# Queries and keys of two head sets from one product each, with the values' projection and a portion of filler moved

## The chip, the cores and the metric

The kernel runs on one core of a Trainium2 chip. The metric is the device time of one execution in microseconds; three runs of the kernel before gave 748.2, 746.93 and 748.02, with a median of 748.02 us. Engines are named as the profile names them: PE (TensorE), DVE (VectorE), ACT (ScalarE), POOL (GpSimd) and SP, which issues most of the transfers.

## What is computed

Two transformer layers over 16 sequences of 256 tokens with 128 features. The change touches the attention of the first layer alone. Cut to that:

```python
xn = _layernorm(x)
qvk = (xn @ Wqvk).reshape(b, s, 3, H, HD)          # H = 16 heads of HD = 8
q, v, k = (qvk[:, :, 0], qvk[:, :, 1], qvk[:, :, 2])
scores = jnp.einsum('bshi,bthi->bsth', q, k)
scores = (scores + mask[None, :, :, None]) / math.sqrt(d)      # causal
weights = jax.nn.softmax(scores, axis=2)
wv = jnp.einsum('bsth,bthi->bshi', weights, v).reshape(b, s, d)
x = x + wv @ Wo + ...                               # and a layer of experts, then a second layer
```

The experts of the first layer, and the retention and experts of the second, run between and after the attention of the sequences.

## The kernel before

**Heads on partitions.** The 16 heads form two sets (s = 0, 1) of eight, and a set lies on the 128 partitions as four groups (j) of 32 rows. A group holds two heads (a = 0, 1), each of 8 rows. A head's score is a product with 32 rows of contraction, and the two heads of a group share the rows of the keys `kU`; the queries `qM` are kept once for each a, with the other head's rows zero. One more row of each group carries the maximum: 1 in `kU`, and the negative row maximum in `qM`. So the product `wts` gives scores with the maximum taken off.

**Making them (lines 418 to 440).** The padded weights `wqk` hold a block of 128 columns for queries or keys and for each set, with 16 of 32 columns used in every group. `products` makes four products a sequence, 128 x 256 each: two into the PSUM bank `pq`, two into `pk`. `keys_and_queries` takes them out: two ACT instructions of 512 columns for `qM`, scaled by a mask `qm`, and one for `kU`, which adds the 1 (`kone`) in row 16. For sequence 0 this last one is on DVE.

**The loop over sequences (lines 1526 to 1571).** Iteration n computes the maxima of sequence n+1 (`top`, with DVE's maximum `nm`) beside the weights of sequence n (`wts`, with the exponential on ACT and the causal select on POOL, both writing `pt`), in six steps. Then comes what I call the seam: the products of sequence n+2 (`project`), the transposes of the maxima `nm` of n+1 into `pm` with their copy `mT` on DVE and four transfers of SP into the rows of `qM` (`top_rows`), the values' projection `pv` of n+2 with its copy `va` on DVE (`project_v`), the two products `av` with the weights (`values`, one for each set, copied by ACT to `sv` and sent out to `num` and `dd`), the division `wv` on DVE (`divide`) that needs the denominators `den` of sequence n-1, and the output projection `po` of n-1, added to `x` by DVE (`project_out`).

**Filler.** All other work (normalization, routing, the first layer's experts, the second layer's steps, loads of weights) is cut into portions; `fill` issues the next portion. There are eight calls in an iteration: one after each of the six steps, one after the second `values`, one after `project_out`. So portion 8n+6 is the one after the second `values`.

**What sets the order.** Instructions go through wrappers (`InOrder`, line 164) that chain them: each engine executes in the order in which this program issues, and SP and POOL issue their transfers in that order too. PSUM is one pool of eight banks handed out in turn (`bank`, line 158).

Line numbers in the profile are mostly 173, the line of the wrapper, so instructions are told apart by the tile that they write and read.

Of the kernel before, what the change touches and what calls it, by code (L numbers as in the profile page):

```python
# [12 lines left out]
F32 = mybir.dt.float32  # L13
BF16 = mybir.dt.bfloat16
I32 = mybir.dt.int32
AF = mybir.ActivationFunctionType
ALU = mybir.AluOpType
AX = mybir.AxisListType
# [3 lines left out]
P = 128  # L22
# [20 lines left out]
def two_layer_kernel(  # L43
# [26 lines left out]
    B, S, D = h.shape  # L70
# [10 lines left out]
    w1pool = ctx.enter_context(tc.tile_pool(name="w1pool", bufs=1))  # L81
    dram = ctx.enter_context(tc.tile_pool(name="dram", bufs=1, space=DRAM))

    def bc(ap, shape):
        return ap.to_broadcast(list(shape))
# [3 lines left out]
    wqvk_sb = w1pool.tile([P, 3 * D], F32)  # L89
# [68 lines left out]
    def bank(shape, name="sc"):  # L158
        return ps.tile(shape, F32, tag="sc", name=name)
# [38 lines left out]
    pe, dve, act, pool, sp = (InOrder(e) for e in (nc.tensor, nc.vector, nc.scalar, nc.gpsimd, nc.sync))  # L198

    def matmul(*args, **kw):  # L200
        return pe.matmul(*args, **kw)

    def transpose(*args):
        return pe.transpose(*args)
# [7 lines left out]
    xnT = big.tile([P, N], F32)  # L212
# [77 lines left out]
    def fill_with(o, value):  # L290
        act.activation(
            o.rearrange("p (k n) -> p k n", n=P),
            bc(ones[0 : o.shape[0]].unsqueeze(1), [o.shape[0], o.shape[1] // P, P]),
            AF.Copy,
            scale=value,
        )


    wqk = w1pool.tile([P, 2, 2, P], F32)
    fill_with(wqk.rearrange("p n s r -> p (n s r)"), 0.0)  # L300


    vas = [w1pool.tile([P, 2, 8, 32], F32, name=f"va{k}") for k in range(3)]
# [17 lines left out]
    for n, c0 in ((0, 0), (1, 2 * D)):  # L321
        for s in range(2):
            dve.tensor_copy(
                wqk[:, n, s, :].rearrange("p (j r) -> p j r", j=4)[:, :, 0:16],
                wqvk_sb[:, c0 + 64 * s : c0 + 64 * s + 64].rearrange("p (j r) -> p j r", j=4),
            )

    r32 = w1pool.tile([P, 32], F32)
    dve.tensor_reduce(r32, ident.rearrange("p (j r) -> p r j", j=4), AX.X, ALU.add)
    km = w1pool.tile([P, 2], F32)  # L330
    dve.tensor_reduce(km, r32[:, 0:16].rearrange("p (a r) -> p a r", a=2), AX.X, ALU.add)
    qm = w1pool.tile([P, 2], F32)
    dve.tensor_scalar(qm, km, 1.0 / math.sqrt(D), None, ALU.mult)
    kone = r32[:, 16:17]

    for t in range(2, 8):
        ln_stats(mv0, t, t)
# [79 lines left out]

    def project(n):

        return keys_and_queries(n, *products(n))  # L420

    def products(n):
        cols = slice(S * n, S * n + S)
        pq = bank([P, 2, S], "pq")
        pk = bank([P, 2, S], "pk")
        for m, o in ((0, pq), (1, pk)):
            for s in range(2):
                matmul(o[:, s, :], lhsT=wqk[:, m, s, :], rhs=xnT[:, cols], start=True, stop=True)
        return pq, pk

    def keys_and_queries(n, pq, pk):
        kU = wk.tile([P, 2, S], F32, tag="kU", name="kU")
        qM = wk.tile([P, 2, 2, S], F32, tag="qM", name="qM")
        for a in range(2):
            act.activation(qM[:, :, a, :], pq, AF.Copy, scale=qm[:, a : a + 1])
        if n == 0:
            dve.tensor_scalar(kU, pk, kone, None, ALU.add)
        else:
            act.activation(kU, pk, AF.Identity, bias=kone)
        return kU, qM, vas[n % 3]  # L440

    def project_v(n):
        pv = bank([P, 2, P], "pv")
        for t in range(2):
            matmul(
                pv[:, t, :],
                lhsT=xnT[:, S * n + t * P : S * n + t * P + P],
                rhs=wqvk_sb[:, D : 2 * D],
                start=True,
                stop=True,  # L450
            )
        va4 = vas[n % 3].rearrange("p k h (d a) -> p (k h) d a", a=4)
        dve.tensor_copy(va4[:, :, :, 0:2], pv.rearrange("p k (h a d) -> p (k h) d a", a=2, d=8))
# [34 lines left out]
    def top_rows(ops, nm):  # L488

        qM = ops[1]  # L490
        pm = bank([16, S], "pm")
        for c in range(2):
            transpose(pm[:, c * P : c * P + P], nm[:, c, :], ident)
        mT = wk.tile([16, S], F32, tag="mT", name="mT")
        dve.tensor_copy(mT, pm)
        for s in range(2):
            for a in range(2):
                h0 = 8 * s + 4 * a
                sp.dma_start(qM[16:P:32, s, a, :], mT[h0 : h0 + 4, :])

    def weights(ops, u, js, pts):

# [51 lines left out]
    def values(ops, s, pts, num, dd):  # L554

        va = ops[2]
        av = bank([P, 2, S], "av")
        for j in range(4):
            matmul(
                av[32 * j : 32 * j + 32].rearrange("p a q -> p (a q)"),  # L560
                lhsT=va[:, 0, 4 * s + j, :],
                rhs=pts[1 + s][:, j, :],
                start=True,
                stop=False,
            )
        for j in range(4):
            matmul(
                av[32 * j : 32 * j + 32, :, P:S],
                lhsT=va[:, 1, 4 * s + j, :],
                rhs=pts[0][:, j, 256 * s : 256 * s + 256].rearrange("p (a q) -> p a q", a=2),  # L570
                start=False,
                stop=True,
            )

        sv = wk.tile([P, 2, S], F32, tag="sv", name="sv")
        act.copy(sv, av)
        sp.dma_start(dd[8 * s : 8 * s + 8, :].rearrange("(a j) q -> j a q", a=2), sv[2:P:32, :, :])
        for a in range(2):
            r = slice(64 * s + 32 * a, 64 * s + 32 * a + 32)
            sp.dma_start(num[r, :], sv[a:P:4, a, :])  # L580
# [641 lines left out]
    def after(portion, *gens):  # L1222
        return [portion, [g for g in gens]]
# [8 lines left out]
    def fill():  # L1232
        for start, gens in beside:
            while gens and start <= at["portion"]:
                try:
                    next(gens[0])
                    break
                except StopIteration:
                    gens.pop(0)
        at["portion"] += 1  # L1240
# [236 lines left out]
    def turn(us):  # L1477

        end()
        at["us"] += us  # L1480
        while at["us"] > 0 and other:
            cost, what, i = other[0]
            if i not in done:
                at["us"] = 0.0
                return
            other.pop(0)
            end()
            what(i)
            at["us"] -= cost
# [11 lines left out]
    ops = {}  # L1501
# [11 lines left out]
    early = products(1)  # L1513
# [2 lines left out]
    dve.tensor_scalar(rev, eid, -1.0, float(E), ALU.mult, ALU.add)  # L1516
    dve.tensor_reduce(hm16, ident.rearrange("p (g j r) -> p j g r", g=4, j=2), AX.XY, ALU.add)
    dve.tensor_reduce(blk16, ident.rearrange("p (h r) -> p h r", h=H1), AX.X, ALU.add)
    ops[1] = keys_and_queries(1, *early)
    project_v(1)  # L1520
    load_router()
    for i in range(2):
# [3 lines left out]
    for n in range(B):  # L1526
        pts = {}
        num = wk.tile([P, S], F32, tag="num", name="num")
        dd = dram.tile([H0, S], F32, tag="dd", bufs=3, name="dd")
        if n + 1 < B:  # L1530
            maxima[n + 1] = wk.tile([P, 2, 16], F32, tag="nm", name="nm")
        sums = denominators(prev[1]) if prev is not None else iter(())
        if n + 1 == B:
            turn(4.0)
        for u in range(3):
            for js, others in (((0, 1), (2, 3)), ((2, 3), (0, 1))):
                parts = [weights(ops[n], u, others, pts)]
                if n + 1 < B:
                    parts.insert(0, top(ops[n + 1], u, js, maxima[n + 1]))
                together(*parts)  # L1540
                next(sums, None)
                fill()
                if n + 1 == B:
                    turn(2.0)
        if n + 2 < B:
            ops[n + 2] = project(n + 2)
        if n + 2 < B:
            top_rows(ops[n + 1], maxima[n + 1])
            project_v(n + 2)
        values(ops[n], 0, pts, num, dd)  # L1550
        if n + 2 == B:
            top_rows(ops[n + 1], maxima[n + 1])
        if prev is not None:
            wv = divide(prev[0], held["den"])
        values(ops[n], 1, pts, num, dd)
        if n + 1 == B:
            held["dens"] = denominators(dd)
            next(held["dens"])
        fill()
        if prev is not None:  # L1560
            project_out(n - 1, wv)
        prev = num, dd
        if n + 1 == B:
            turn(2.0)
        fill()
        if n + 1 == B:
            turn(2.0)
        if n == 8:
            fW1_sb = big.tile([P, E, FF], F32, tag="WV", name="fW1_sb")
            fW2_sb = big.tile([P, E, NFC, D], F32, tag="xnw", name="fW2_sb")  # L1570
            beside.append(after(0, load1()))
# [108 lines left out]
```

## Time and profile before

The profiled execution took 747.65 us; its span, from the first to the last instruction, is 745.9 us.

| | |
|---|---|
| median of three runs | 748.02 us |
| profiled execution, its span | 747.65 us, 745.9 us |
| granted TensorE clock, mean | 0.991 |
| attention of the 16 sequences | from about 7 to about 400 us |
| products pq and pk of one sequence | 8 records, 1.83 us from the first to the next work's start |
| ACT qM, kU, 512 columns each | 684 ns, 695 ns |
| DVE copies mT, va | 0.41 us, 0.43 us |

A line of the timeline gives the start in microseconds from the span's start, the time until the last of a merged run of instructions ends, the engine, the operation with out<-in, the shape and the count; in brackets stands how long the engine had been idle and what released it. Records of TensorE overlap, so the time from one start to the next is what a product costs.

### The profile page before, as it was taken

To read this page: it belongs to the slowest core of one execution; us is meant where nothing else is said; L and a number is where in the kernel's file an instruction comes from. 1 tells how busy PE (TensorE), PEld (TensorE's weight loads), DVE (VectorE), ACT (ScalarE), POOL (GpSimd) and SP (SyncE) were. 2 spreads that over 40 slices of the span, in tenths; PEclk is the share of its full clock that TensorE was granted. 3 is DMA by queue.
4 is the path that set the end of the run, shared out by engine and by line. 5 is a ranking of instruction groups with operands and counts; after the bars stand their busy time and mean duration, and the time that the engine had idled before them with its cause. 6 is when DMAs were issued, how large, how long until landed. Compare 5 with 4: busy or idle time off the path is not lost.

```text
span 745.9 us, 14847 instructions
## 1 busy us (share of the span) xinstructions
PE 716.3 (96%) x5645; PEld 478.9 (64%) x5648; DVE 397.2 (53%) x1066; ACT 361.3 (48%) x714; POOL 274.5 (37%) x475
## 2 busy tenths in 40 slices
PE   8899989999899999999999899999999999999997
PEld 6557556766555666656565566666776676767675
DVE  8675876766657666586452656753323233223222
ACT  5477535555576676876666444233232322232222
POOL 1253345787556557666372413344000000121000
PEclk9899999999999999999999999999999999999999
DMA  4114464233333645413222121232000000323111
GB/s 125 23 57 130 131 188 117 39 47 43 52 73 88 153 104 142 88 36 54 65 51 56 23 65 43 80 79 35 1 29 2 0 1 1 43 34 38 35 38 43
DMA packets 79312, 45.73 MB, mean 61 GB/s; under 512 B 17112, under 2 KB 74656, under 8 KB 79232
## 3 DMA queue, kind: packets, MB, share of 16 engines
q1 hardware_dynamic: 62432, 34.84, 16.3%
q0 software_dynamic: 16800, 9.83, 10.3%
q8 instruction: 50, 0.82, 0.5%
q14 instruction: 30, 0.25, 0.1%
HBM read 24.97 MB, written 17.31 MB: 57 GB/s over the span
## 4 chain that ended last, share of the span: by engine, by line
PE 75%; DVE 12%; DMA 4%; POOL 3%; ACT 3%; issue 2%; SPq 1%; DVEq 0%; ACTq 0%; POOLq 0%
PE py L173 20%; PE ph L173 18%; PE top L173 8%; PE av L173 5%; PE wts L173 4%; DVE nm L173 4%; PE po L173 3%; PE pq L173 2%; DMA x<-ytab 2%; PE pk L173 2%; PE pret L173 2%; PE psc L173 1%; PE plog L173 1%; PE pb L173 1%; DVE st L173 1%
## 5 line engine op out<-in xcount | busy, mean ns | idle before, releaser
L173 ACT ACTIVATE hT<-ph,b1T 128x512 f32<-128x512 f32 (+1 forms) x134 | 90.1, 678 | 169.7 <-PE ph L173 154.0
L173 PEld LDWEIGHTS py<-fW_sb,hT 128*128 128x128 f32 x1328 | 155.2, 192 | 21.3 <-issue 19.8
L173 PE MATMUL py<-fW_sb,hT 128*128 128x128 f32 x1328 | 157.7, 276 | 0.0
L173 PE MATMUL ph<-xnT,fW_sb 128*128 128x512 f32 x320 | 147.4, 601 | 0.0
L173 DVE TENSOR_REDUCE nm<-top 128x2 f32<-128x512 f32 (+1 forms) x192 | 122.3, 681 | 32.6 <-PE wts L173 19.1
L173 ACT ACTIVATE pt<-wts 128x512 f32<-128x512 f32 x192 | 104.8, 599 | 66.3 <-PE wts L173 48.6
L173 PE MATMUL wts<-qM,kU 32*128 32x512 f32 (+1 forms) x512 | 121.2, 530 | 0.7 <-DVE come L173 0.5
L173 POOL TENSOR_SCALAR_AFFINE_SELECT pt<-pt 128x512 f32<-128x512 f32 (+1 forms) x96 | 82.7, 884 | 100.2 <-ACT pt L173 93.1
L173 PE MATMUL top<-kU,qM 32*128 32x256 f32 (+1 forms) x1024 | 110.9, 349 | 0.5 <-issue 0.4
L173 PEld LDWEIGHTS ph<-xnT,fW_sb 128*128 128x128 f32 x320 | 58.0, 192 | 61.9 <-issue 57.4
L173 PEld LDWEIGHTS top<-kU,qM 32*128 32x128 f32 x1024 | 73.6, 190 | 30.1 <-issue 26.5
L173 DVE SCALAR_TENSOR_TENSOR x<-py,gate,x 128x128 f32<-128x128 f32 x160 | 48.6, 346 | 70.7 <-PE py L173 70.7
L173 DVE TENSOR_SCALAR hT<-ph,b1T 128x512 f32<-128x512 f32 (+1 forms) x38 | 26.6, 708 | 96.7 <-ACT hT L173 58.1
L173 POOL DMA_DIRECT2D x<-acc x8 | 10.4, 1366 | 157.9 <-issue 115.0
L173 PEld LDWEIGHTS wts<-qM,kU 32*128 32x128 f32 x512 | 48.7, 189 | 7.5 <-DVE nm L173 2.1
L173 POOL TENSOR_SCALAR_AFFINE_SELECT s<-s 128x1024 f32<-128x1024 f32 x32 | 34.7, 1109 | 37.5 <-ACT s L173 37.5
L173 PE MATMUL av<-pt,va 128*32 128x256 f32 (+1 forms) x512 | 45.1, 489 | 2.5 <-POOL pt L173 2.1
L173 PE MATMUL top<-cmask,ident_bf 128*128 128x256 bf16 (+1 forms) x189 | 44.5, 316 | 0.5 <-DVE nm L173 0.5
L173 ACT COPY s<-psc 128x512 f32<-128x512 f32 x64 | 32.7, 602 | 4.7 <-PE psc L173 4.7
L173 PEld LDWEIGHTS av<-pt,va 128*32 128x32 f32 x512 | 14.7, 109 | 27.6 <-issue 19.7
L173 ACT COPY sv<-av 128x512 f32<-128x512 f32 x32 | 18.5, 590 | 24.4 <-issue 10.5
L173 PE MATMUL pq<-xnT,wqk 128*128 128x256 f32 (+1 forms) x80 | 26.5, 445 | 1.4 <-ACT xnT L173 1.4
(251 smaller groups left out, 932.7 us busy)
## 6 DMA issues: line engine op xcount, KB each, us to landing
ytab<-zeros SPq DMA_DIRECT2D x16, 256.0 KB
x<-ytab POOLq DMA_DIRECT2D x16, 256.0 KB
fW_sb<-in_L_ffn_W_dram SPq DMA_DIRECT2D x16, 256.0 KB
xtab<-xnw SPq DMA_DIRECT2D x8, 272.0 KB
num<-sv SPq DMA_DIRECT2D x64, 32.0 KB
den<-di SPq DMA_DIRECT2D x16, 128.0 KB
xtab<-xn SPq DMA_DIRECT2D x8, 256.0 KB
acc<-zeros SPq DMA_DIRECT2D x8, 256.0 KB
```

Source lines behind the costliest of these rows:

```text
L173: ins = f(*args, **kw)
```

## The change

Queries of both sets come out of one product, keys out of another: the columns of `wqk` interleave the sets and heads (row 4d + 2s + a in a group), all 128 columns are used, and masks pick what belongs to a set and head when the product is taken out. For queries there are four masks (one for each s and a); for keys a mask per set clears the row that carries the 1 and adds it. That row is 2 for set 0 and 0 for set 1. Both products go into one PSUM bank, `pqk`. They are taken out in six instructions of 256 columns. At the seam `project_v` goes ahead of `top_rows`, and the filler portion 8n+6 goes between the first and the second `values`, for n = 0 to 13.

```diff
-    wqk = w1pool.tile([P, 2, 2, P], F32)
-    fill_with(wqk.rearrange("p n s r -> p (n s r)"), 0.0)
+    wqk = w1pool.tile([P, 2, P], F32)
...
             dve.tensor_copy(
-                wqk[:, n, s, :].rearrange("p (j r) -> p j r", j=4)[:, :, 0:16],
-                wqvk_sb[:, c0 + 64 * s : c0 + 64 * s + 64].rearrange("p (j r) -> p j r", j=4),
+                wqk[:, n, :].rearrange("p (j d s a) -> p s j a d", j=4, s=2, a=2)[:, s],
+                wqvk_sb[:, c0 + 64 * s : c0 + 64 * s + 64].rearrange("p (j a d) -> p j a d", j=4, a=2),
             )
...
-    km = w1pool.tile([P, 2], F32)
-    dve.tensor_reduce(km, r32[:, 0:16].rearrange("p (a r) -> p a r", a=2), AX.X, ALU.add)
-    qm = w1pool.tile([P, 2], F32)
-    dve.tensor_scalar(qm, km, 1.0 / math.sqrt(D), None, ALU.mult)
-    kone = r32[:, 16:17]
+
+    qm = w1pool.tile([P, 4], F32)
+    dve.tensor_reduce(qm, r32.rearrange("p (d c) -> p c d", c=4), AX.X, ALU.add)
+    dve.tensor_scalar(qm, qm, 1.0 / math.sqrt(D), None, ALU.mult)
+
+    kone = [r32[:, 2:3], r32[:, 0:1]]
+    km = w1pool.tile([P, 2], F32)
+    for s in range(2):
+        dve.tensor_scalar(km[:, s : s + 1], kone[s], -1.0, 1.0, ALU.mult, ALU.add)
...
-        pq = bank([P, 2, S], "pq")
-        pk = bank([P, 2, S], "pk")
-        for m, o in ((0, pq), (1, pk)):
-            for s in range(2):
-                matmul(o[:, s, :], lhsT=wqk[:, m, s, :], rhs=xnT[:, cols], start=True, stop=True)
-        return pq, pk
-
-    def keys_and_queries(n, pq, pk):
+        pqk = bank([P, 2, S], "pqk")
+        for m in range(2):
+            matmul(pqk[:, m, :], lhsT=wqk[:, m, :], rhs=xnT[:, cols], start=True, stop=True)
+        return pqk
+
+    def keys_and_queries(n, pqk):
         kU = wk.tile([P, 2, S], F32, tag="kU", name="kU")
         qM = wk.tile([P, 2, 2, S], F32, tag="qM", name="qM")
-        for a in range(2):
-            act.activation(qM[:, :, a, :], pq, AF.Copy, scale=qm[:, a : a + 1])
-        if n == 0:
-            dve.tensor_scalar(kU, pk, kone, None, ALU.add)
-        else:
-            act.activation(kU, pk, AF.Identity, bias=kone)
+        for s in range(2):
+            for a in range(2):
+                c = 2 * s + a
+                act.activation(qM[:, s, a, :], pqk[:, 0, :], AF.Copy, scale=qm[:, c : c + 1])
+            if n == 0:
+                dve.tensor_scalar(kU[:, s, :], pqk[:, 1, :], km[:, s : s + 1], kone[s], ALU.mult, ALU.add)
+            else:
+                act.activation(kU[:, s, :], pqk[:, 1, :], AF.Identity, scale=km[:, s : s + 1], bias=kone[s])
...
-                sp.dma_start(qM[16:P:32, s, a, :], mT[h0 : h0 + 4, :])
+                sp.dma_start(qM[2 - 2 * s : P : 32, s, a, :], mT[h0 : h0 + 4, :])
...
         if n + 2 < B:
+            project_v(n + 2)
             top_rows(ops[n + 1], maxima[n + 1])
-            project_v(n + 2)
         values(ops[n], 0, pts, num, dd)
+        if n + 2 < B:
+            fill()
...
-        fill()
+        if n + 2 >= B:
+            fill()
```

More of the change, by code (lines that the diff above doesn't have):

```diff
@@ L418, in project @@
     def project(n):
-        return keys_and_queries(n, *products(n))
+        return keys_and_queries(n, products(n))
     def products(n):
         cols = slice(S * n, S * n + S)
-        pq = bank([P, 2, S], "pq")
-        pk = bank([P, 2, S], "pk")
-        for m, o in ((0, pq), (1, pk)):
-            for s in range(2):
-                matmul(o[:, s, :], lhsT=wqk[:, m, s, :], rhs=xnT[:, cols], start=True, stop=True)
-        return pq, pk
-    def keys_and_queries(n, pq, pk):
+        pqk = bank([P, 2, S], "pqk")
[3 more added lines that the diff above has]
+    def keys_and_queries(n, pqk):
         kU = wk.tile([P, 2, S], F32, tag="kU", name="kU")
         qM = wk.tile([P, 2, 2, S], F32, tag="qM", name="qM")
-        for a in range(2):
-            act.activation(qM[:, :, a, :], pq, AF.Copy, scale=qm[:, a : a + 1])
-        if n == 0:
-            dve.tensor_scalar(kU, pk, kone, None, ALU.add)
-        else:
-            act.activation(kU, pk, AF.Identity, bias=kone)
+        for s in range(2):
[6 more added lines that the diff above has]
+                act.activation(kU[:, s, :], pqk[:, 1, :], AF.Identity, scale=km[:, s : s + 1], bias=kone[s])
         return kU, qM, vas[n % 3]
@@ L1518, in two_layer_kernel @@
     dve.tensor_reduce(blk16, ident.rearrange("p (h r) -> p h r", h=H1), AX.X, ALU.add)
-    ops[1] = keys_and_queries(1, *early)
+    ops[1] = keys_and_queries(1, early)
     project_v(1)
```

## The prediction

> **What bounds the kernel now.** I read the busy shares first, then the chain of waits, then the timeline of single iterations.
>
> ```profile
> PE 716.3 (96%) x5645; PEld 478.9 (64%) x5648; DVE 397.2 (53%) x1066; ACT 361.3 (48%) x714; POOL 274.5 (37%) x475
> ...
> PE 75%; DVE 12%; DMA 4%; POOL 3%; ACT 3%; issue 2%; SPq 1%; DVEq 0%; ACTq 0%; POOLq 0%
> ```
>
> TensorE is busy 96% of the span but carries only 75% of the chain that ended last. The other quarter, with 12% on VectorE, is where TensorE work taken away may leave the end where it is. The change touches the prologue and the stretch between two attention loops (the seam), so I read the seam. Iteration n=6, the plainest:
>
> ```profile
> 176.08 1.13 PE L173 MATMUL pq<-xnT,wqk 128*128 128x256 f32 x4
> 177.05 1.03 PE L173 MATMUL pk<-xnT,wqk 128*128 128x256 f32 x4
> 177.91 0.38 PE L173 MATMUL pm<-ident,nm 128*16 128x128 f32 x2
> 178.13 0.61 PE L173 MATMUL pv<-wqvk_sb,xnT 128*128 128x128 f32 x4
> 178.33 0.41 DVE L173 COPY mT<-pm 16x256 f32<-16x256 f32 x1 [0.77 <-PE pm L173]
> 178.67 2.79 PE L173 MATMUL av<-pt,va 128*32 128x512 f32 x32
> 178.77 2.35 SPq L173 DMA_DIRECT2D qM<-mT  x4
> ```
>
> TensorE runs on without a hole; the maxima go out through VectorE (mT) and four SP transfers that the next loop's `wts` products need. Here the four landing records end at 182.47 and the `wts` of the second set start at 183.91, so 1.4 us are in hand. Over all seams that margin (last landing to first `wts` of the second set) runs from 0.14 us (n=0 and n=3) to several us. n=7 is the seam with the longest holes:
>
> ```profile
> 195.80 0.42 DVE L173 TENSOR_TENSOR wv<-num,den 128x256 f32<-128x256 f32 x1 [1.02 <-DMA den<-di]
> 200.46 0.29 DVE L173 BATCH_NORM_STATS2 st<-x 128x6 f32<-128x128 f32 x1 [4.24 <-DMA x<-ytab]
> ...
> 197.81 1.50 PE L173 MATMUL av<-pt,va 128*32 128x512 f32 x16 [2.07 <-POOL pt L173]
> 199.24 0.71 PE L173 MATMUL po<-wo_sb,wv 128*128 128x128 f32 x4
> ```
>
> VectorE computes `wv` at 195.80, and only then stands 4.24 us waiting for the expert rows (x<-ytab) before the statistics `st`. TensorE's `po` at 199.24 needs `wv` and not `st`.
>
> **The products.** Each fp32 product is two TensorE records. pq and pk are four products, 8 records, 0.97 + 0.86 us from start to start; half of them go: 0.86 us for each of 16 sequences, 13.8 us of TensorE at most.
>
> **The evacuations.** ScalarE had three instructions of 512 columns (qM 684 ns, kU 695 ns), and gets six of 256. No row has this form. A plain copy costs 590 ns at 512 columns and 372 at 256; a scale operand adds about 95 (684 against 590), scale and bias together about 210 (xn 486 against vm 272, both 128 wide). So 465 and 580 ns; neighbours overlap by 0.11 (two qM take 1.26). Six: 4x0.465 + 2x0.58 - 5x0.11 = 2.5 us against 1.84, +0.65 us per sequence (between 0.4 and 1.0). At seven of the fourteen seams ScalarE idles 1.2 to 2.2 us before `sv`, which hides it; if that cover is gone, `sv` and what ScalarE does for the filler come 0.65 later.
>
> **Values' projection ahead of pm.** pm waited for the last maximum `nm`, which at n=6 ends 1.48 us after the seam's start. With one product pair gone, the seam reaches pm at 0.97 + 0.46 = 1.43 instead of 1.83: the moved pv is nearly all the cover that is needed, about 0.1 is lost. But on VectorE the `va` copy (0.43) now stands ahead of mT. Where VectorE idles for pm, it fits into the gap; where VectorE is behind, mT and its transfers go 0.35 later.
>
> **The moved filler** is the one that decides. It stands between the two `values`, ahead of `divide` too. So all VectorE work of that portion now comes before `wv`, and `po` waits behind it. Its SP and POOL transfers move ahead of the second set's dd and num, whose readers come over 2 us later; I cost that at nothing. Per seam (+ is later), by the rows of that seam, ScalarE's extra included:
> - n=0: VectorE full of statistics to 42.5, mT later by 0.35; the landing was already last (44.21 for a `wts` at 44.35): **+0.35**.
> - n=1: 0.76 of the product saved, 2 us of landing in hand; ScalarE's six evacuations stand before the filler's xnT copy: **-0.5**.
> - n=2: saving eaten by `va` ahead of mT (VectorE busy until 78.9; landing margin 0.47): **0**.
> - n=3: transfers of maxima held by table writes on SP until 101.50: no saving. But the search's `by` copy (103.61) no longer stands behind a `wv` that waited 1.90 for its denominators, so POOL's `within` starts some 1.7 earlier and a 0.96 us TensorE wait for it goes: **-0.8**.
> - n=4, n=5: the filler is an expert's pb, pa, pw. VectorE's sb, ehT and search take 2.76 from 126.62 on, and now precede `wv`. n=4: pb starts at 122.0, ScalarE's tanh ends at 123.9, VectorE 126.7, `wv` 127.05, `po` 127.1 against 126.85: **+0.2**. n=5 likewise, with py and two ys ahead of the tanh: `po` 158.0 against 157.26: **+0.7**.
> - n=6: nothing on VectorE in this portion: **-0.8**.
> - n=7: `st` waits for a transfer that POOL issues at 195.82 in either order, so it ends at 201.3; `wv` 201.7, `po` 201.75 instead of 199.24. That is 2.5 later; the next loop, where VectorE's lateness cost about 1.5 (199.79 to 210.74 is 10.95, against 8.83 of loop work and 0.55 of pT), gives part back: **+1.1** (0.5 to 2.5).
> - n=8, 9, 10, 13: `po` or the next product is held by the same thing as before (prob behind ScalarE's vm; xnT behind ScalarE; gate behind POOL's gp; prob): **0** each.
> - n=11: `wv` waited for denominators until 292.69 with the gates' work behind it; that work now fits in the wait, and the state product no longer stalls: **-0.5**.
> - n=12: before, `wv` was done at 313.6, `po` came at 316.87. Now st, ks, prob (behind ScalarE's vm at about 316) and two statistics come first: `wv` 317.6, `po` 317.8: **+0.9**.
>
> **The prologue, and a rule against the change.**
>
> ```profile
> 8.66 1.27 ACT L173 ACTIVATE qM<-pq,qm 128x512 f32<-128x512 f32 x2 [1.22 <-PE pq L173]
> 9.91 0.72 DVE L173 TENSOR_SCALAR kU<-pk,r 128x512 f32<-128x512 f32 x1
> 10.55 0.16 DVE L173 TENSOR_SCALAR nv<-mv 128x6 f32<-128x6 f32 x1
> ```
>
> VectorE is the chain here: from 2.96 to 20.2 it hardly rests, so the product saving is worth nothing and all it gains counts. Two more small operations (0.2 apart) and kU in two of 256 columns (+0.1) are +0.45 by the rows alone, with ScalarE and VectorE side by side. The Trainium skill (PSUM — Partial Sum Buffer, section on bank collisions) says that two engines must not be in one PSUM bank and partitions at once, even in different columns, and be kept apart by semaphores. Before, ScalarE read pq and VectorE pk, two banks; now both halves are in one bank, and the program as built makes them take turns: qM, qM, then kU, then qM, qM, then kU. By that rule VectorE stands while ScalarE does its second pair: kU at 10.26 to 10.68, the pair to 11.6, kU to 12.1, `nv` at 12.05 instead of 10.55: **+1.5**. I take the rule; no row of this trace shows the turn-taking.
>
> **Sum:** 1.5 + 0.35 - 0.5 + 0 - 0.8 + 0.2 + 0.7 - 0.8 + 1.1 - 0.5 + 0.9 = **+2.15 us**. The profiled execution took 747.65 (span 745.9, 1.75 around it): 749.8. Its time is 0.37 below the median 748.02, so against runs I say **750.0 us**. Uncertain by half a microsecond at some ten seams and by the two ends at n=7 and the prologue: own range 747.5 to 753.
>
> **Rivals.**
> - *The filler's VectorE work costs nothing* (say, inputs ready sooner than I count), and only the landings of the maxima limit. Then n=4, 5, 6, 8, 12, 13 give 0.86, 0.54, 0.8, 0.82, 0.2, 0.82, n=7 and 10 0 and 0.36; with the others as above and prologue +1.5 the sum is -4.35, or 743.7 against the runs. Its point: in n=4, 5, 8, 12 and 13 the filler's last VectorE row must end within the 1.36 us of the second `values`. For it: TensorE is 96% busy, and VectorE idles 1 to 4 us at most seams; against: that idle time is spent waiting for the filler's own inputs. If TensorE alone decided, 734.
> - *ScalarE surfaces.* At n=8 to 13 it is 60 to 80% busy, and 0.65 more per sequence holds PSUM banks and the exponentials. If half of 14x0.65 shows beside the sum: +6.7, 754.7. Against: between 20 and 345 us no group of TensorE's waits for ScalarE comes to more than 2.6 us in total now.
> - *It comes out even:* prologue without turns (+0.45) and n=7 at its low end: +0.5, 748.5.
> - *The change doesn't do what it says:* excluded for the products, 64 fewer TensorE products' records (2 products x 2 records x 16) must appear. The filler "between the sets" does move, but it covers a wait of TensorE at n=7 only, with nothing on TensorE in that portion.
>
> **Chances:** forecast 0.52, filler-free gain 0.20, ScalarE 0.12, even 0.16. Range to hold 8 in 10: 743.5 to 755. About 0.2% (1.5 us) is what a measurement tells from no change: faster 0.20, same 0.21, slower 0.59.
>
> **What would show it.** Right: 64 fewer TensorE records; in the prologue VectorE idle between two kU, `nv` near 12; at n=7 `st` before `wv` and `po` near 202 less the shift; at n=12 `wv` behind two `st`; `mT` after `va`. Wrong: a `wv` that ends before `po` could start at n=4, 5, 12; kU halves back to back; waits of `top` or `wts` for ScalarE in the loops after n=8.

## The result, and the profile after

The changed kernel takes 756.94 us in the median of six runs (755.05 to 760.71), the kernel before in six runs beside them 747.51 (746.64 to 749.0): a ratio of 1.0124, 95% interval 1.0092 to 1.0156. A second session gave 758.0 us and 1.0109 (1.0081 to 1.0137). It is slower by about 9 us; I had said 2.

The profiled execution took 755.05 us, the fastest of the six, with a span of 753.3 us; so 7.4 us of the loss lie in the profile. The first lines of the page of the changed kernel, and its chain of waits:

```profile
PE 708.2 (94%) x5579; PEld 468.0 (62%) x5584; DVE 398.4 (53%) x1069; ACT 370.4 (49%) x760; POOL 273.6 (36%) x475
...
PE 68%; DVE 13%; DMA 5%; POOL 5%; ACT 4%; issue 3%; SPq 1%; DVEq 0%; ACTq 0%; POOLq 0%
```

The change does what it says: TensorE is busy 8.1 us less (66 records fewer are shown, 64 were to go; some records can be missing). Its share of the chain falls from 75% to 68%, while the span grows: what was taken from it did not come out as time, and waits took its place.

To see where, I measured each seam from the start of its products to the fifth `wts` record of the next loop, and each loop from there to the next products, in the timelines of both profiles. "Forecast" is the term of the prediction's sum.

| | forecast | seam | loop before it |
|---|---|---|---|
| prologue | +1.5 | +2.30 | |
| n=0 | +0.35 | +0.33 | +0.64 |
| n=1 | -0.5 | -0.52 | +0.35 |
| n=2 | 0 | +0.21 | 0 |
| n=3 | -0.8 | -0.07 | 0 |
| n=4 | +0.2 | +1.69 | +0.40 |
| n=5 | +0.7 | +0.95 | 0 |
| n=6 | -0.8 | -0.52 | -0.02 |
| n=7 | +1.1 | +3.39 | 0 |
| n=8 | 0 | -0.53 | -0.73 |
| n=9, n=10 | 0 | +0.04 | -0.34 |
| n=11 | -0.5 | +1.12 | -0.23 |
| n=12 | +0.9 | +1.09 | -0.04 |
| n=13 | 0 | -0.53 | -0.60 |
| sum | +2.15 | +8.95 | -0.57 |

The prologue is measured to the fifth `wts` record of the first loop. After n=13 another 1.0 us is given back, which leaves the 7.4.

The plain seam, n=6, in the timeline of the changed kernel:

```profile
182.34 1.13 PE L173 MATMUL pqk<-xnT,wqk 128*128 128x256 f32 x4
183.31 0.61 PE L173 MATMUL pv<-wqvk_sb,xnT 128*128 128x128 f32 x4
...
184.29 0.40 DVE L173 COPY mT<-pm 16x256 f32<-16x256 f32 x1
```

`pqk` to `pv` is 0.97 us, and `mT` comes 1.95 us after the seam's start instead of 2.25. This seam gains 0.52 us. Now n=7, the same view:

```profile
201.01 1.29 POOL L173 DMA_DIRECT2D x<-ytab  x1 [2.33 <-DMA x<-ytab]
...
205.55 0.29 DVE L173 BATCH_NORM_STATS2 st<-x 128x6 f32<-128x128 f32 x1 [5.80 <-DMA x<-ytab]
...
206.48 0.43 DVE L173 TENSOR_TENSOR wv<-num,den 128x256 f32<-128x256 f32 x1
206.96 1.22 PE L173 MATMUL po<-wo_sb,wv 128*128 128x128 f32 x4 [1.65 <-DVE wv L173]
```

POOL issues the second transfer of expert rows at 201.01, `st` waits for its landing 5.80 us, `wv` stands behind `st`, and TensorE waits for `wv`: the mechanism that the prediction named. But `po` takes 1.22 us where it took 0.71. The granted clock is at half there. The view of busy time by stretches shows it; its columns are the stretch, its length, then the busy time and number of instructions of PE, PEld, DVE, ACT and POOL, the granted TensorE clock, the DMA share and GB/s:

```profile
12.40:15.82 3.42, 1.68 (x26) 1.05 (x26) 3.15 (x13) 1.67 (x5) 0.00 (x0) 1.00 0.00 0
15.82:19.21 3.39, 3.39 (x24) 2.41 (x24) 2.34 (x5) 1.26 (x4) 0.00 (x0) 0.50 0.02 5
118.21:121.63 3.42, 0.49 (x8) 0.00 (x0) 3.28 (x9) 1.08 (x2) 3.03 (x4) 1.00 0.83 228
121.63:125.03 3.40, 3.02 (x9) 2.40 (x10) 0.39 (x1) 0.72 (x2) 2.92 (x5) 0.50 0.25 73
200.13:203.55 3.42, 1.05 (x20) 0.27 (x16) 0.00 (x0) 1.39 (x4) 1.94 (x2) 1.00 0.25 50
203.55:206.96 3.41, 1.77 (x16) 0.25 (x8) 1.26 (x5) 0.59 (x1) 0.00 (x0) 0.50 0.55 81
```

Read them in pairs: a stretch of 3.4 us in which TensorE has little to do (1.68, 0.49, 1.05 us) runs at full clock, and the stretch after it, in which there is work, at half. The wait is paid twice. Over the seams of n=4 and n=7 the granted clock is 0.90 and 0.74 on average, where the kernel before has 1.00 in both. The prediction has no term for this.

### The profile page after: what moved, and what is told of

Same layout as the page of the kernel before. It is cut to its first block, busy times and chain, and to the rows that moved or that the text cites. A ratio compares the mean times of both kernels' runs of the same rounds, so it can differ in the third digit from the quotient of the medians.

```text
span 753.3 us, 14751 instructions
## 1 busy us (share of the span) xinstructions
PE 708.2 (94%) x5579; PEld 468.0 (62%) x5584; DVE 398.4 (53%) x1069; ACT 370.4 (49%) x760; POOL 273.6 (36%) x475
## 4 chain that ended last, share of the span: by engine, by line
PE 68%; DVE 13%; DMA 5%; POOL 5%; ACT 4%; issue 3%; SPq 1%; DVEq 0%; ACTq 0%; POOLq 0%
PE py L173 20%; PE ph L173 17%; PE top L173 7%; PE wts L173 4%; PE av L173 3%; DVE nm L173 3%; PE po L173 3%; DMA x<-ytab 3%; PE pret L173 1%; POOL pt L173 1%; PE psc L173 1%; PE plog L173 1%; PE pT L173 1%; DVE st L173 1%; ACT pt L173 1%
## 5 line engine op out<-in xcount | busy, mean ns | idle before, releaser
L173 PE MATMUL ph<-xnT,fW_sb 128*128 128x512 f32 x320 | 145.8, 595 | 0.0
L173 PE MATMUL top<-kU,qM 32*128 32x256 f32 (+1 forms) x1024 | 113.4, 356 | 1.6 <-DVE kU L173 1.4
L173 PE MATMUL av<-pt,va 128*32 128x256 f32 (+1 forms) x512 | 48.3, 498 | 2.6 <-POOL pt L173 2.6
L173 DVE TENSOR_TENSOR x<-po,x 128x256 f32<-128x256 f32 (+1 forms) x24 | 12.3, 514 | 34.4 <-PE po L173 30.5
L173 ACT ACTIVATE qM<-pqk,qm 128x256 f32<-128x256 f32 x64 | 27.1, 482 | 6.8 <-PE pqk L173 5.6
```

The source lines that it names most:

```text
L173: ins = f(*args, **kw)
```

## The experiments

Two theories of the result, then. **M**: `po` waits for `wv` behind the filler's VectorE work, as forecast, only longer. **C**: TensorE has less to do around its waits, the granted clock falls to half more often, and that is the rest. Rivals: ScalarE's six evacuations (S), the PSUM banks (T for the prologue, R for the ring of banks), the filler's transfers. Times are medians; ratios are to the kernel before in the same session (748.9 to 749.7 us there, more runs and a wider spread than in the first one). "Clock" is the median over a kernel's runs of the run's mean granted clock; the kernel before has 0.990 to 0.993.

### The filler back, the filler alone, `wv` ahead of it, part of it

```diff
         values(ops[n], 0, pts, num, dd)
-        if n + 2 < B:
-            fill()
...
-        if n + 2 >= B:
-            fill()
+        fill()
```

> The changed kernel with the filler portion 8n+6 back behind the second values product; the one product each, the six evacuations and the values' projection ahead of pm stay. Theory M (the filler's VectorE work ahead of wv is most of the loss, with the half-clock spells that its holes bring): what stays is the prologue's +1.6 to 2.3 us and a saving of up to 0.76 us at seams with a margin for the maxima; 746 us (743 to 750), wv ends before po could start at n=4, 5, 12, and at n=7 po does not wait for st. Theory S (the six evacuations on ScalarE, or va ahead of mT, are the loss): the loss stays, 754 us or more.

751.95 us, 1.0033 (1.0015 to 1.0051), clock 0.982. Neither number was met: most of the loss goes with the filler, so S is refuted as its main cause, but 2.5 us stay where I expected a gain. At the plain seams the saved product does show in its profile (-0.85, -0.87, -0.87 and -0.86 us at n=6, 8, 10 and 13); the stretch ahead of the first seam (+2.55), n=4, n=7 and the loop of n=10 take more back, the last with a granted clock of 0.91 where it was 1.00.

The filler alone is the opposite edit, the moved `fill` put into the kernel before:

> The kernel before with the filler portion 8n+6 moved between the two values products, nothing else changed. Theory M: po waits for wv behind the filler's VectorE work at n=4, 5, 7 and 12, prologue as before; 754 us (752 to 757). Theory S: moving the filler alone is nothing, 747 to 748.5 us.

756.26 us, 1.0085 (1.0058 to 1.0112), clock 0.991: the filler's place alone costs 6.4 us, at the clock of the kernel before. Its timeline at n=4:

```profile
124.83 0.69 DVE L173 SCALAR_TENSOR_TENSOR sb<-sb,pb 128x512 f32<-128x512 f32 x1 [2.75 <-ACT sb L173]
...
127.69 0.42 DVE L173 TENSOR_TENSOR wv<-num,den 128x256 f32<-128x256 f32 x1
...
128.26 0.68 PE L173 MATMUL po<-wo_sb,wv 128*128 128x128 f32 x4 [1.23 <-DVE wv L173]
```

VectorE waits 2.75 us for the expert's tanh, with the denominators there since 118.64, does 2.86 us of the expert's work, and TensorE stands 1.23 us for `wv`. In the kernel before, `wv` went ahead of that wait, and `po` followed TensorE's own work:

```profile
122.07 0.42 DVE L173 TENSOR_TENSOR wv<-num,den 128x256 f32<-128x256 f32 x1
126.62 0.69 DVE L173 SCALAR_TENSOR_TENSOR sb<-sb,pb 128x512 f32<-128x512 f32 x1 [4.13 <-ACT sb L173]
...
126.85 0.71 PE L173 MATMUL po<-wo_sb,wv 128*128 128x128 f32 x4
```

n=5, 7, 11 and 12 show the same order. At n=1, 6, 8 and 13, where no VectorE work is in the portion, the seam is still 0.33 us longer (last section).

`wv` ahead of the filler, in the changed kernel:

```diff
-        if n + 2 < B:
-            fill()
...
         if prev is not None:
             wv = divide(prev[0], held["den"])
+        if n + 2 < B:
+            fill()
         values(ops[n], 1, pts, num, dd)
```

> The changed kernel with wv (divide) put ahead of the moved filler; the filler itself stays between the two values products. Theory M in its narrow form (VectorE's order before wv is the price): po no longer waits at n=4, 5, 7, 12, nearly all of the loss goes but the prologue's, 747 us (744 to 750). Rival within it (the moved filler costs by its transfers on SP and POOL and by its TensorE and ScalarE work, not by wv): 753 us or more, with the gather of the first expert still waiting about 4.5 us at n=4.

750.37 us, 1.0004 (0.9979 to 1.0029), clock 0.982. One instruction's place on VectorE takes away nearly the whole loss, with the clock still at 0.982. The narrow form of M holds; the filler's transfers, which stay where the change put them, are not the price. In its timeline at n=4 `po` no longer waits for `wv`:

```profile
125.19 0.40 DVE L173 TENSOR_TENSOR wv<-num,den 128x256 f32<-128x256 f32 x1
...
131.04 0.71 PE L173 MATMUL po<-wo_sb,wv 128*128 128x128 f32 x4
```

The move undone at five seams only (`n not in (4, 5, 7, 11, 12)` added to the condition):

> The changed kernel with the portion 8n+6 moved at all seams but n=4, 5, 7, 11 and 12, where it is back behind the second values product. Theory M (po behind the filler's VectorE work at these five seams is the loss): seams of n=4, 5, 7, 11, 12 shorter by about 5.5 us in sum than in the changed kernel, 751.5 us. Rival (the move costs something at every seam, as by splitting the narrow products av in two blocks): 754 to 755 us.

751.4 us, 1.0019 (0.9995 to 1.0042), clock 0.982, as M said: those five seams carry the filler's loss.

### The products alone, and the values' projection

The kernel with the filler back, and `top_rows` ahead of `project_v` again:

> The one product each and the six evacuations alone: filler back behind the second values product and the maxima's transposes ahead of the values' projection, as in the kernel before. If the values' projection ahead of pm is worth what I costed (0.1 to 0.4 us of TensorE at seams where pm waits for nm, against mT 0.35 later at n=0), this is within 1 us of the kernel with the filler back, 751 to 753 us, with pm waiting 0.3 to 0.9 for nm at the plain seams and the n=0 seam shorter by 0.35. Rival (va ahead of mT costs at many seams): 749 us or less.

749.54 us, 0.9998 (0.9977 to 1.0019), clock 0.986. This is nearer the rival's number than mine. One product each and six evacuations together come to nothing in the times. S falls as a cause of the loss: TensorE's waits for ScalarE between 20 and 360 us add up to 2.6 us in this profile and to 2.7 in the one before. The saved product goes elsewhere: TensorE now comes to the transposes too early, and `pm` waits for the maxima `nm` 9.7 us in ten waits, where it was 2.5 us in three. Against the kernel with the filler back (1.0033) the values' projection ahead of the maxima seems to cost 2.4 us, more than the n=0 seam's 0.33 that I had costed, though the two intervals overlap. Between the two the clock differs too (0.982 and 0.986), and which is the cause of which was not taken apart.

### PSUM banks

Sequence 0 in two banks, in the changed kernel:

```diff
-        pqk = bank([P, 2, S], "pqk")
+        if n == 0:
+            pqk = [bank([P, S], "pq"), bank([P, S], "pk")]
+        else:
+            both = bank([P, 2, S], "pqk")
+            pqk = [both[:, 0, :], both[:, 1, :]]
```

> The changed kernel with sequence 0's queries and keys in two PSUM banks, all other sequences as changed. Theory T (ScalarE and VectorE take turns in the one bank, +1.6 us in the prologue, and the half-clock spell at 15.8 us comes of it): nv at about 11.0 instead of 12.15 us after the span's start, the loop begins 1.1 to 2.3 us earlier, 755 us against 756.9. Rival (the turns are covered by the statistics that VectorE owes anyway): nv earlier, the loop's start not, 757 us.

756.61 us, 1.0086 (1.0054 to 1.0117). The prologue in the timeline of the changed kernel:

```profile
10.25 0.54 DVE L173 TENSOR_SCALAR kU<-pqk,km,r 128x256 f32<-128x256 f32 x1
...
10.82 0.84 ACT L173 ACTIVATE qM<-pqk,qm 128x256 f32<-128x256 f32 x2 [1.13 <-DVE kU L173]
...
11.69 0.54 DVE L173 TENSOR_SCALAR kU<-pqk,km,r 128x256 f32<-128x256 f32 x1 [0.91 <-ACT qM L173]
12.15 0.16 DVE L173 TENSOR_SCALAR nv<-mv 128x6 f32<-128x6 f32 x1
```

and of the one with two banks:

```profile
10.24 0.96 DVE L173 TENSOR_SCALAR kU<-pk,km,r 128x256 f32<-128x256 f32 x2
...
11.12 0.16 DVE L173 TENSOR_SCALAR nv<-mv 128x6 f32<-128x6 f32 x1
```

The turns are there, ScalarE idle 1.13 us for VectorE and VectorE 0.91 for ScalarE, and two banks take them away: `nv` comes 1.03 us earlier, and the first seam 1.4. In the times it cannot be told from the changed kernel, since the intervals overlap.

Two banks for every sequence, with the filler back (condition `True`):

> The filler back behind the second values product, and for every sequence queries and keys each in a PSUM bank of their own, so that the ring of eight banks turns as in the kernel before; the one product each, the six evacuations and the values' projection ahead of pm stay. Theory R (with a bank less per sequence wts and top come to banks that other work still holds, 0.5 us in the loop of n=6 and 1.6 at n=10; and the prologue's turn-taking is 1.0): 749 us against the 752 of the kernel with the filler back, the loops of n=6 and n=10 as long as before, seams of n=1, 6, 8, 13 shorter by 0.5 to 0.9. Rival (what the loops lose is ScalarE's longer evacuations or chance): only the prologue's 1.0 goes, 751 us, and the loops of n=6 and n=10 stay longer.

754.59 us, 1.0061 (1.004 to 1.0082). Theory R is refuted: the loop of n=6 is still 0.50 longer and that of n=10 1.72, and the seam of n=11 is longer by 2.8. In two of the three lies a half-clock spell of 3.4 us, which gives up 1.7: the granted clock is 0.91 over the loop of n=10 and 0.87 over the seam of n=11, where the kernel before has 1.00. What brings the spells there, the 0.50 and the rest stay open. The same with six idle products in the prologue:

> The kernel with two banks for every sequence, and six products of ones with ones into an unused bank in the prologue, where TensorE stands between the first maxima's products and the transposes pT; they add no result. Theory C (the granted clock falls to half at 13 to 20 us because TensorE has less to do there than before, and that costs 1.0 to 1.2 us): no half-clock spell there, the loop begins 1 us earlier than without them, 748 us if that kernel takes 749. Rival (the spell does not depend on this hole, or it costs nothing, VectorE's chain being the longer): same time as without them.

753.75 us, 1.0059 (1.0039 to 1.008): no difference by itself. Its profile has no half-clock spell before 25 us, but the one without the added products had none before 22 us either. Inconclusive.

Two banks for sequence 0, products alone:

> The one product each and six evacuations alone (filler and the maxima's transposes where they were), with queries and keys of sequence 0 in two PSUM banks. Theory T (turn-taking in the prologue costs 1.0 us of the start): 748.5 us against 749.5 for the products alone. Rival (in the runs the prologue's start is lost in the half-clock spells, or the bank more puts the ring into another position with waits of its own): 749.5 us or more.

750.2 us, 1.0021 (0.9996 to 1.0046), clock 0.984: the rival; the earlier start is not seen in the time.

### The clock

The added products write ones times ones where the next product overwrites them:

```diff
         pxs = bank([P, CAP], "pxs")
+        for _ in range(6 if e == 0 else 0):
+            matmul(pxs[:, 0:P], lhsT=ones, rhs=ones, start=True, stop=True)
...
         av = bank([P, 2, S], "av")
+        for _ in range(idle):                  # 8 for the second set of n=7
+            matmul(av[:, 0, 0:P], lhsT=ones, rhs=ones, start=True, stop=True)
```

and six likewise in the first `pT` bank of the prologue. In the changed kernel:

> The changed kernel with the same added products ahead of the same three waits. Theory C: clock from 0.983 to about 0.989, 754 us (752.5 to 755) against 757; what is left above the kernel before is the filler's seams. Rival: 756 us or more.

752.43 us, 1.0034 (1.0017 to 1.0051), clock 0.991. Twenty useless products make the kernel 4.5 us faster, by the median of the first session. The two kernels side by side in one session:

> The changed kernel unchanged, beside the next one on the same chip. If the lost clock is a part of the loss: 757 us at a mean clock of 0.983 to 0.985, as before.

> The changed kernel with the added products at all three places, again. If the lost clock is a part of the loss: 752 to 754 us at a mean clock near 0.990, 3 us or more under the changed kernel of the same session. If the 752.4 was the session's: within 1.5 us of it.

758.0 us (1.0109, clock 0.981) against 753.55 (1.0059, interval 1.0041 to 1.0078, clock 0.993): 4.45 us again. In the kernel that is kept busy, the stretch that had TensorE busy for 1.68 us reads

```profile
12.40:15.82 3.42, 3.22 (x38) 2.47 (x38) 3.15 (x13) 1.69 (x5) 0.00 (x0) 1.00 0.00 0
```

and no half-clock stretch follows. At n=7 the added products run for 2.05 us, and 0.35 us of the wait for `pt` is left; the wait for `wv` after it stays, and a spell of 3.4 us follows instead of 6.8. At n=4 a wait of 2.14 us for the gather is left, and its spell stays. This profile is of the slowest of the 22 runs (754.61 us, clock 0.986) and holds 20.5 us of half clock, as the profile of the changed kernel does: that the clock rises is read from all runs, not from this one.

The same products in the kernel with the products alone and two banks for sequence 0, and in the kernel before:

> The same kernel with products of ones with ones into banks that the next products overwrite, ahead of three waits of TensorE: six in the prologue before pT, six before the first expert's pxs (n=4), eight before the second av of n=7; they add no result. Theory C (the time that the products gain is given back because waits with less TensorE work around them let the granted clock fall to half: time follows lost clock at 0.6 to 0.8 us per us): mean clock from about 0.986 to 0.990 or more, no half-clock spell at 13 to 20, 122 and 204 us, 746 us (744.5 to 747.5). Rival (the spells come elsewhere then, or the added products stand in the way): clock and time as without them, 748.5 us or more.

747.08 us, 0.9963 (0.9943 to 0.9983), from 1.0021: 4.3 us. The clock rose less than I expected, from 0.984 to 0.986 (0.984 to 0.988 in the mean).

> The kernel before with the same added products ahead of the same three waits. Theory C says that its clock, 0.990 to 0.991, is less often lost at these places (its profile shows spells at 22, 108 and 428 us): 748 us (747 to 749), a gain of at most 1 us. Rival (the added products help every kernel alike, so that the lost clock is no part of what the change did): a gain as large as for the kernel with the products alone, 2 us or more.

747.49 us, 0.9971 (0.9952 to 0.9989), clock 0.993: 2.2 us, so the kernel before loses clock too, but half as much. This lies nearer the rival's number than mine: by this count about half of the 4.5 us that the changed kernel gets back is owed to the change.

Each place by itself, in the changed kernel:

> The changed kernel with the eight added products ahead of the second av of n=7 alone. The wait there is the longest (2.4 us for pt, and then 1.65 for wv), with a spell of 6.8 us behind it in the profile: if the clock is lost there above all, 754.5 us and a mean clock of 0.987; if the places share it alike, 755.5; if n=7 has no part, 757.

> The changed kernel with the six added products ahead of pxs of the first expert (n=4) alone. A wait of 3.1 us and a spell of 3.4 us behind it: 755.5 us if the places share it alike; 757 if six products are too few for this wait.

> The changed kernel with the six added products ahead of pT in the prologue alone. Spells at 15.8 and 26.1 us in the profile: 755.5 us if the places share it alike; 757 if VectorE's chain of maxima sets the prologue's end in any clock.

757.5, 757.03 and 759.03 us (1.0109, 1.0098, 1.014), clocks 0.984 to 0.986: none does anything that can be told, and all three together give 4.5 us. At which place the clock is lost stays open. In the profile of the one kept busy at n=4 the spell at 121.6 is gone and that seam's +1.69 falls to +0.55, so the places work where they stand; why that does not reach the end was not found.

### Joined

The cheapest pieces together: one product each, maxima before the values' projection, `wv` ahead of the moved filler, all three waits kept busy.

> The one product each, the maxima's transposes ahead of the values' projection as before, the filler between the two values products but with wv ahead of it, and the added products at all three places. If the parts add up (products alone 0, wv ahead of the filler no loss, kept busy -2 to -4): 746 us (744 to 748), under both kernels. Rival (the filler between the sets costs 0.33 at every seam even so): 748.5 us or more.

747.36 us, 0.9969 (0.9949 to 0.999), clock 0.990. It is faster than the kernel before by 0.3%, and no faster than the kernel before with the same added products (0.9971). In the times, the change's one product each has no measurable worth in any of these.

## Why the prediction was wrong

The direction was right, and so was the filler's mechanism, `po` behind `wv` behind the portion's VectorE work. The size was off by 7 us, and 756.94 lies outside the range, which ended at 755. (The sum's own terms give 750.2 against the runs; the 750.0 is a slip without weight.) By its steps:

**What held.** The prologue's turn-taking: `kU`, pair, `kU`, `nv` were forecast at 10.26, up to 11.6, up to 12.1, and 12.05, and came at 10.25, 11.66, 12.23 and 12.15. The Trainium skill's rule on bank collisions (PSUM — Partial Sum Buffer) was the right one to take; by the rows alone `nv` would have been 11.0, and with two banks it is 11.12. The prologue as a whole came 2.3 us later and not 1.5; `nv` accounts for 1.6 of it, and a half-clock spell at 15.8 us follows. ScalarE's six evacuations: 2.48 us at n=6 of the kernel with the filler back (181.51 to 183.99), forecast 2.5. The seams of n=0, 1 and 12 within 0.2 us, n=5 and 6 within 0.3. The rival that the filler's VectorE work costs nothing is refuted by the filler alone (1.0085). The rival "ScalarE surfaces" finds no support: the products alone are at 0.9998, and TensorE waits no longer for ScalarE than before.

**The step that failed: the sum knows no clock.** It prices every TensorE row at the duration that it had before, and puts what the change does to the granted clock at nothing, without a reason. Half-clock spells show in the profile of before too (22.4, 107.8 and 428.6 us, 13.65 us in all, against 20.5 after); I had read the mean clock of 0.991 and not asked what takes it down. Over 220 runs of the kernel before beside the experiments, a run's time rises by 0.75 us for each microsecond of lost clock (750 us times one minus its mean clock; correlation 0.75). This is a correlation, but it lets the kernels be read at equal clock. The table has how far their runs lie from that line in the mean (uncertain by 0.2 to 0.8 us, the first number by 1.7), and their mean clock:

| | mean clock | us from the line |
|---|---|---|
| changed kernel, first and second time | 0.982, 0.981 | +3.5, +3.6 |
| changed kernel, kept busy, first and second time | 0.992, 0.991 | +3.7, +4.9 |
| filler alone | 0.991 | +7.5 |
| filler back | 0.982 | -2.2 |
| products alone | 0.985 | -2.8 |
| kernel before, kept busy | 0.993 | -0.1 |

So the added products work through the clock: at equal clock the changed kernel is no faster with them. The one product each, with its six evacuations, does gain some 2 to 3 us at equal clock, and in the times loses them again to a lower clock. And at equal clock the change costs 3.5 us, or up to 4.9 by the kernels kept busy, where the sum had 2.15; the clock's fall from 0.990 in the mean to 0.981 or 0.982 adds about 5 (an estimate: 7 us more lost, at 0.75). The added products give a smaller share: they take 4.5 us off the changed kernel and 2.2 off the kernel before, so 2.3 of the loss is the change's clock by that count. Between these two, 2.3 and 5 of the 7 us missed, the runs don't decide; the rest is in the terms below.

**Terms mis-sized beside it,** by the profile:
- *n=3, "-0.8, a TensorE wait for `within` goes".* That wait did go, and POOL's `within` came 1.5 us earlier against the shift. But the gather of the first expert needs the last of the table writes (xtab) too, which SP issues. Before, its indices were ready at 110.6 and the last write landed at 113.68, with the gather at 114.76: the write was already the last thing.

```profile
110.05 0.72 SPq L173 DMA_DIRECT2D xtab<-xnw  x1
...
114.76 1.24 POOL L173 DMA_INDIRECT xk<-xtab,idx  x1 [1.96 <-DVE slot L173]
```

  After, with the seam 3.3 us later, the write lands at 117.21, no earlier than before by its own measure:

```profile
114.18 0.63 SPq L173 DMA_DIRECT2D xtab<-xnw  x1
...
118.28 1.24 POOL L173 DMA_INDIRECT xk<-xtab,idx  x1 [4.53 <-DMA ytab<-zeros]
...
121.78 0.45 PE L173 MATMUL pxs<-ident,xk 128*128 128x128 f32 x1 [3.08 <-DMA xk<-xtab,idx]
```

  (The brackets at the gather name other transfers and VectorE, by the last signal that the view saw; POOL's queue stood on the write's signal, until 113.71 before and 117.24 after.) I asked what the removed stall costs, and not what is late next. TensorE's holes there, 0.35 and 0.91 us before, became one of 3.08 us, and half clock follows.
- *n=4, +0.2.* +1.69 in the profile. About 1.0 of it is `pqk` and `pv` at half clock, 2.44 us from the first to `pm` instead of 1.41 at n=6, and with the spell gone the seam is at +0.55 (kept busy at n=4 alone). The rest is `wv`, later than forecast.

```profile
122.73 1.92 PE L173 MATMUL pqk<-xnT,wqk 128*128 128x256 f32 x4
124.44 0.90 PE L173 MATMUL pv<-wqvk_sb,xnT 128*128 128x128 f32 x4
125.17 0.38 PE L173 MATMUL pm<-ident,nm 128*16 128x128 f32 x2
```

- *n=7, +1.1.* `po` came 2.0 us later in its seam (9.56 us from the seam's start instead of 7.58), forecast 2.5; the rest of the seam, at half clock, lost another 1.4. I had the next loop give back 1.4, and it gave 0.73.
- *n=11, -0.5, "that work now fits in the wait for the denominators".* +1.12. The work didn't fit: the first `st` waited for its rows 1.57 us (0.77 before), everything of VectorE came later, and `wv`, 6.77 us after the seam's start before, came after 8.37.

```profile
293.71 0.29 DVE L173 BATCH_NORM_STATS2 st<-x 128x6 f32<-128x128 f32 x1 [1.57 <-DMA x<-ytab]
...
301.62 0.41 DVE L173 TENSOR_TENSOR wv<-num,den 128x256 f32<-128x256 f32 x1
302.18 0.68 PE L173 MATMUL po<-wo_sb,wv 128*128 128x128 f32 x4 [1.35 <-ACT sq L173]
```

- *n=8 and 13, 0.* They gained 0.53 each: there, with no VectorE work in the portion that `wv` needs to await, the saved product does show. The loops before them gave back another 0.73 and 0.60 of what earlier seams had lost.

**The gain that was expected** at seams is real where it was forecast (n=1, 6: half a microsecond in the profile). With the filler back and the maxima first it comes to nothing in the times, at a clock of 0.986 instead of 0.991. That is in keeping with theory C and with the table above; but what lowers the clock in that kernel, at which wait, is argued, not shown.

## What to carry to other kernels

An instruction on an in-order engine that someone else waits for belongs ahead of work that waits for something itself: here the place of one 0.42 us division decided 6 us (756.6 to 750.4 us in one session). Where a stall is to go, look for the input that arrives next, with its landing time, before the gain is booked. And where TensorE is nearly always busy, price its waits with the clock that they cost: take work away around a wait, and the work after it may run at half rate.

## What the runs showed of the hardware that was not expected

**The clock follows the stretch before.** In 20 profiles I cut the time between 10 and 700 us into stretches of 3.41 us, on the grid on which the half-clock spells begin (they last 3.4, 6.8 or, once, 10.2 us). Of 47 stretches at full clock with TensorE busy less than half, 44 were followed by half clock; of some 500 between 50% and 90%, 51; of over 3300 above 90%, none. The Trainium skill (TensorE: Matmul & The Clock Gate, Part 1) tells of such a free-running window of 4096 cycles, 3413 ns, and the spells' length agrees. Its rule of thumb, no gaps over 3.4 us, is too mild for this kernel: in the prologue a wait of 1.68 us was enough, in a stretch with TensorE busy 1.68 of 3.42 us. The grid doesn't start with the kernel: in the two profiles of the changed kernel the first spell begins at 15.8 and at 13.5 us, and they hold 20.5 and 34.2 us of half clock. So the same waits cost more clock in one execution than in another, and the lost clock goes with over half of the variance of the runs (743.5 to 755.2 us for the kernel before; correlation 0.75).

**Two blocks of narrow products cost more apart.** Between the two blocks of `av` (32 columns of weights each) the moved filler puts products with 128 columns. At n=6 the kernel with the filler alone spends 1.43 + 1.08 + 1.43 + 0.55 us from the first `av` to the next `top`, the kernel before 2.72 + 0.99 + 0.45 for the same products: 0.33 us more, with two changes of shape more. It shows at every seam with nothing else in the way (+0.33 or +0.34 at n=1, 6, 8 and 13). That the change of shape is the reason was not tested by itself.

**One bank, two engines** cost 1.03 us in the prologue, where each of two engines stood about a microsecond for the other.
